# A residual addition moved from VectorE to accumulating transfers on GpSimd's queue

## The chip, the cores and the metric

The kernel runs on one core of a Trainium2 chip. The metric is device time in microseconds (us) for one execution of the whole program; a lower time is better. A core has a matrix engine (TensorE, PE in the profile; PEld is its loading of weights), a vector engine (VectorE, DVE), a scalar engine (ScalarE, ACT), GpSimd (POOL) and a queue engine (SyncE, SP). Each takes its instructions in the order in which the program lists them and waits, in that order, for the semaphores of other engines and of transfers (DMAs). Work is held in SBUF, 128 partitions wide; PE writes to PSUM, of which this kernel uses five accumulator tiles of 128 x 512 (`ACC = 5`).

## The reference

The input x has 4 batches of 1024 rows and 2048 columns. From a small matrix product come six modulation vectors per batch (`sa, ca, ga, sb, cb, gb`). Then two residual steps follow:

```
h = layernorm(x) * (1 + ca) + sa
x = x + ga * conv(h)            # long convolution along the 2048 columns, plus D[0]*h
h = layernorm(x) * (1 + cb) + sb
x = x + gb * (h @ W.T + bias + low-rank update)
```

The change concerns the second line, the addition of x to the gated convolution, and what the layer norm of the third line needs of that sum: its mean and its variance along each row.

## The kernel before

**Stages.** The 4096 rows of x are 32 tiles of 128 rows, numbered r = 0 to 31. In a first stage (about 0 to 190 us) the modulation vectors are computed from `wmod` and the convolution's tables are made; tiles 0 and 1 are convolved there without gate (`EARLY = 2`). In the second stage (about 190 to 912 us) tiles 2 to 31 are convolved, one after the other; a turn of that loop (lines 1143 to 1181) is called block r here. Into the blocks up to about r = 24 the kernel mixes "fill" work: the merge of W with its low-rank update (`merge`, line 483: PE products `lps` at L502, taken from PSUM by VectorE at L504, split by ACT and DVE at L529 and L530, stored as `wcd`) and the remaining modulation sections (`modps`, L320). In the third stage (about 912 us to the end) 16 pairs of tiles go through the feed-forward product (`ffn_unit`, L829), twice, once for each half of the columns.

**One block.** `conv_mm` (line 657) multiplies in two passes, q = 0 and q = 1; q = 1 has 2.6 times the columns of q = 0. Each pass has three families of PE products: family 0 into the PSUM tile `ya`, copied by ACT to `qs` (L695); family 2 into `yb`; family 1, which goes on accumulating in `ya`. VectorE then makes one half of a row's 1024 elements from `yb` (L704: add `qs`; L706: times the row's scale `rsx` and the gate `gat`) and the other half from `ya` (L713: times `rsx` and `gat`, here called the gate of the pass). At L714 VectorE adds x to the 1024 columns of the pass and gives out the row sums through its accumulator (`sums`).

**After a block.** `conv_post` (line 732) of tile r stores y to DRAM (`x1d`, L734), turns the two row sums into minus the mean (L736), and lets ACT square the sum with that bias and accumulate the variance (L739). The squares that ACT gives out are not used; they are written over the x tile, which then is free.

**Buffers.** x has four buffers in SBUF (`x{r % 4}`), y two. So the tile x of r + 3 is loaded (`x_load`, L614) into the buffer of tile r - 1, and its load comes after `conv_post` of r - 1. Of x VectorE makes row statistics (`stats`, L566 `bn_stats`, four instructions a tile, then L567), for two tiles at a time. They end in a small PE product (`qp`, L581), a PE transpose (`svp`, L606) and scales `cas` and `rsx` that the preparation of the tile (`conv_prep`) and its gate need. The transposed copy `xt`, from which the convolution's operand is made, is a separate load (L620).

**What sets the order.** `conv_mm` calls `tick()` at ten places in a block: after each of the six families, and in the middle of each family of pass 1 (numbers 3, 5 and 7), and number 9 after the block. `PLAN` (line 891) has a string for each of them. "P" is `conv_post` of the block before and the load of x for r + 3; "N" a step of the next tile's preparation; "S" a step of fill work; "T" (even r only) the first part of the statistics for r + 2 and r + 3, "t" one of the two later parts (`qp`; then `svp`). The framework places each engine's instructions in one fixed order from this program order and from its own estimates. SP issues all large transfers, in order, with at most eight semaphores in turn; an issue that waits holds up those behind it. POOL's own queue has 28 transfers in the whole kernel, all before 146 us, and a few memsets.

At the end of the second stage, the weights of the second and third product of the third stage are loaded into the four x buffers (`XW`, line 1082): those of the third product (`w5`) into the buffers of tiles 30 and 31.

Of the kernel before, what the change touches and what calls it, by code (L numbers as in the profile page):

```python
# [12 lines left out]
F32 = mybir.dt.float32  # L13
F16 = mybir.dt.float16
BF16 = mybir.dt.bfloat16
I32 = mybir.dt.int32
AF = mybir.ActivationFunctionType
ALU = mybir.AluOpType
AX = mybir.AxisListType
MUL, ADD, SUB = ALU.mult, ALU.add, ALU.subtract  # L20
# [4 lines left out]
P = 128  # L25
D = 2048
# [9 lines left out]
class Net:  # L36
# [515 lines left out]
    def stats(self, pl, rs_, out):  # L552
        nc, v = self.nc, self.nc.vector
        n, b = len(rs_), rs_[0] // 8
        tt = v.tensor_tensor

        def T(shape, name, dt=F32):
            if name in ("cas", "rsx", "sw"):
                return pl["sm1" if n == 1 else "sm"].tile([P, *shape], dt, tag=f"{name}{n}", name=name)
            return pl["sm"].tile([P, 2, *shape[1:]], dt, tag=name, name=name)[:, 0:n]  # L560

        mv = T((n, 2), "mv")
        for i, r in enumerate(rs_):
            st = pl["sm"].tile([P, 4, 6], F32, tag="st1", name="st1")
            for q in range(4):
                v.bn_stats(st[:, q], self.xs[r][:, ds(512 * q, 512)])  # L566
            v.bn_aggr(mv[:, i], st)  # L567
        mean, var = mv[:, :, 0], mv[:, :, 1]
        m2, qb = T((n,), "m2"), T((n,), "qb", BF16)
        tt(m2, mean, mean, MUL)  # L570
        tt(qb, m2, var, ADD)
        ve, t, rs = T((n,), "ve"), T((n,), "t"), T((n,), "rs")
        v.tensor_scalar(ve, var, 0.25, 0.25e-5, MUL, ADD)
        nc.scalar.activation(t, ve, AF.Sqrt)
        v.reciprocal(rs, t)
        tt(ve, ve, rs, MUL)
        tt(var, ve, t, ADD)
        v.reciprocal(rs, var)
        yield
        qp = self.tps.tile([P, n], F32, tag="t", name="qp")  # L580
        self.lastq = nc.tensor.matmul(qp, self.ones, qb, start=True, stop=True)  # L581
        bd = T((n,), "bd")
        nc.scalar.activation(bd, qp, AF.Sqrt, bias=self.tiny, scale=self.cm2[:, b : b + 1])
        inv, s2 = T((n,), "inv"), T((n,), "s2")
        v.tensor_scalar(inv.bitcast(I32), bd.bitcast(I32), 0x7F800000, None, ALU.bitwise_and)
        v.tensor_scalar(s2.bitcast(I32), inv.bitcast(I32), 0x7F800000, None, ALU.bitwise_xor)
        cas, rsx = T((n, NC), "cas"), T((n,), "rsx")
        cab = self.ca[:, :, b].unsqueeze(1).to_broadcast([P, n, NC])
        tt(cas, cab, s2.unsqueeze(2).to_broadcast([P, n, NC]), MUL)  # L589
        tt(rsx, rs, inv, MUL)  # L590
        full = self.spt[rs_[0] // 2 % 2][:, rs_[0] % 2 : rs_[0] % 2 + n]
        if rs_[0] % 8 < 4:
            nc.gpsimd.memset(full, 0.0)
        f3 = full[:, :, ds(18 * b, 18)].rearrange("p n (i k j) -> p n i k j", i=2, k=3)
        w = T((n, 2), "w")
        s2b = s2.unsqueeze(2).to_broadcast([P, n, 2])
        tt(w, mv, s2b, MUL)
        for k in range(3):
            for i in range(n):
                v.tensor_copy(f3[:, i, :, k], w[:, i].unsqueeze(2).to_broadcast([P, 2, 3]))  # L600
            if k < 2:
                tt(w, w, f3[:, :, :, k, 0], SUB)
        yield
        tp = self.tps.tile([P, n, P], BF16, tag="t", name="svp")
        for i in range(n):
            nc.tensor.transpose(tp[:, i], full[:, i], self.identb)  # L606
        sw = T((n, P), "sw", BF16)
        nc.scalar.copy(sw, tp)
        out.update({r: (cas[:, i], rsx[:, i : i + 1], sw[:, i]) for i, r in enumerate(rs_)})
        yield  # L610

    def x_load(self, pl, r):
# [44 lines left out]
    def conv_mm(self, pl, r, hs, x, st, tick, early, pace, hook=None):  # L657
        nc, v = self.nc, self.nc.vector
        hc, hs = hs
        y = yv = None  # L660
        if not early:
            gv = self.gat.rearrange("p (j e t) -> p j e t", e=2, t=P)
            mv = self.gm.rearrange("k (j e t) -> k j e t", e=2, t=P)
        rsx = st[1]
        sums = self.sums[:, r]

        def rank(ps, jj, e):
            if not early:
                nc.tensor.matmul(ps, st[2], mv[:, jj, e, :], start=False, stop=False, skip_group_check=True)

        def family(ps, f, q, first):
            pf = ps.rearrange("p j t -> p (j t)")
            last = 4 * q + 3
            for i in range(last + 1):
                o = P * max(0, i - 4 * q)
                k0 = P * max(0, 4 * q - i)
                with pace(3 * (512 - o)):
                    for x, z in ((0, 0), (0, 1), (1, 0)):
                        h = hs[x][:, i] if f == 0 else hc[x][:, 2 * i + 2 - f]
                        self.lastc = nc.tensor.matmul(  # L680
                            pf[:, o:512], h, self.kf[f][z][:, ds(k0, 512 - o)],
                            start=first, stop=(i == last and (x, z) == (1, 0)), skip_group_check=True,
                        )
                        first = False
                if i == (last - 1 if hook else 0) and f:
                    rank(ps, slice(4 * q, 4 * q + 4), f // 2)
                if i == 3 and q == 1:
                    tick()

        for q in range(2):  # L690
            jj = slice(4 * q, 4 * q + 4)
            pa = self.acc.tile([P, 4, P], F32, tag="a", name="ya")
            family(pa, 0, q, True)
            qs = pl["t"].tile([P, 4, P], F32, tag="qs", name="qs")
            self.lasta = nc.scalar.copy(qs, pa)  # L695
            tick()
            pb = self.acc.tile([P, 4, P], F32, tag="a", name="yb")
            family(pb, 2, q, True)
            if y is None:
                if hook:  # L700
                    hook()
                y = pl["y"].tile([P, D], F32, tag="y", name="y")
                yv = y.rearrange("p (j e t) -> p j e t", e=2, t=P)
            self.lastv = v.tensor_tensor(yv[:, jj, 1, :], pb, qs, ADD)  # L704
            if not early:
                v.scalar_tensor_tensor(yv[:, jj, 1, :], yv[:, jj, 1, :], rsx, gv[:, jj, 1, :], MUL, MUL)  # L706
            tick()
            family(pa, 1, q, False)
            sl = ds(1024 * q, 1024)
            if early:  # L710
                nc.scalar.copy(yv[:, jj, 0, :], pa)
            else:
                v.scalar_tensor_tensor(yv[:, jj, 0, :], pa, rsx, gv[:, jj, 0, :], MUL, MUL)  # L713
                v.scalar_tensor_tensor(y[:, sl], y[:, sl], 1.0, x[:, sl], MUL, ADD, accum_out=sums[:, q : q + 1])  # L714
            tick()
        return y, sums

# [11 lines left out]
            v.scalar_tensor_tensor(y[:, sl], y[:, sl], st[1], self.gat[:, sl], MUL, MUL)  # L729
            v.scalar_tensor_tensor(y[:, sl], y[:, sl], 1.0, x[:, sl], MUL, ADD, accum_out=sums[:, q : q + 1])  # L730

    def conv_post(self, pl, r, x, y):
        nc, v = self.nc, self.nc.vector
        STQ(nc).dma_start(out=self.x1d[r], in_=y)  # L734
        mn = self.ln2[:, r, 0:1]
        v.tensor_scalar(mn, self.sums[:, r, 0:1], self.sums[:, r, 1:2], -1.0 / D, ADD, MUL)  # L736
        if r < EARLY:
            x = pl["mrg"].tile([P, D], BF16, tag="wct", name="lsj")
        nc.scalar.activation(x, y, AF.Square, bias=mn, accum_out=self.sqs[:, r : r + 1])  # L739
        if r % 8 == 7:  # L740
            sl = slice(r - 7, r + 1)
            self.rstd(pl["sm8"], self.sqs[:, sl], self.ln2[:, sl, 1], 8, "r2", 1.0 / D)
            v.tensor_tensor(self.ln2[:, sl, 0], self.ln2[:, sl, 0], self.ln2[:, sl, 1], MUL)
# [144 lines left out]

MR = 2
ACC, TPS = 5, 2  # L890
PLAN = ("PNSL", "NL", "NSL", "NTL", "SL", "StL", "SL", "StL", "SL", "SSL")
PLAN2 = ("", "", "", "", "N", "N", "N", "N", "", "")
PLAN3 = ("PS", "", "S4", "", "NS", "NS", "NS5", "NS", "S", "SS")
LPLAN = ("LL", "LL", "LL", "LL", "L", "0", "")
# [4 lines left out]
EARLY = 2  # L899
# [6 lines left out]
def STQ(nc):  # L906
    return nc.sync
# [7 lines left out]
def net(ctx: ExitStack, tc: tile.TileContext, io):  # L915
    nc = tc.nc
    k = Net(ctx, tc, io)
# [11 lines left out]
    pl = {}  # L929
# [1 line left out]
    msm = pool(right, "msm", 1, "right")  # L931
    pl["x"] = pool(p2, "p1x", 1)
    k.kpool = pool(left, "kt", 1)
    k.sums = k.kpool.tile([P, 32, 2], F32, tag="sums", name="sums")
    k.identb = k.kpool.tile([P, P], BF16, tag="identb", name="identb")
    nc.gpsimd.tensor_copy(k.identb, k.ident)
    k.ones = k.kpool.tile([P, P], BF16, tag="ones", name="ones")
# [54 lines left out]
    xs, xts, hs, sts, ys = {}, {}, {}, {}, {}  # L992
# [148 lines left out]
    post = None  # L1141
    sgen = [iter(())]
    for r in range(EARLY, 32):
# [34 lines left out]
        y, _ = k.conv_mm(pl, r, hs.pop(r), xs[r], sts[r], tick, False, behind if r == EARLY else none, late if r == EARLY else None)  # L1178
        tick()
        take(nxt, 9)  # L1180
        post = (r, xs.pop(r), y)
    k.conv_post(pl, *post)
    take(lgen, 10)
    gens = [next_left(1)]
# [94 lines left out]
```

## Time and profile before

| quantity | value |
|---|---|
| median of the runs shown (3) | 2137.91 us (2133.5 to 2143.52) |
| the profiled execution's own time | 2131.82 us |
| span of that execution in the profile | 2130.0 us, so 1.8 us lie around it |
| granted PE clock over the span | 0.986 of full |
| GpSimd busy | 24.2 us in 53 instructions |
| bytes moved by DMA | 512.97 MB, of it 1.65 MB on GpSimd's queue |

The profile is one execution, taken by the hardware profiler. Busy time counts an engine's instructions; a wait is put down to the semaphore that was raised last. Ends of PE's instructions are modelled, so a busy PE may still wait a little. In the views of groups a row gives line, engine, operation, tiles written and read, shapes and count, then the busy time and the mean duration, then idle time just before and who ended it. In the views of time a row gives start, length, engine, line and tiles. In the views by stretch each row has the stretch, its length, the busy time of PE, PEld, DVE, ACT and POOL with their counts, then the granted PE clock, the share of the 16 DMA engines' time and GB/s.

### The profile page before, as it was taken

The numbers are of one execution on the slowest core, as the hardware profiler recorded it, in microseconds if no ns is written. First come the engines' busy times: TensorE is split into PE (matmuls) and PEld (weight loads), VectorE is DVE, ScalarE is ACT, GpSimd is POOL, SyncE is SP. The second block draws the span as 40 slices with busy tenths as digits, with TensorE's granted clock in tenths as the row PEclk, the third lists the DMA queues.
The fourth block names the chain that finished last, engine by engine and source line by source line (L and its number), as shares of the span: only waits on it lengthen the run. The fifth ranks groups of instructions, "written<-read, shape, count | busy, mean of one in ns | idle before, by whom it ended". The sixth has DMA issues, their size and how long they took to land.

```text
span 2130.0 us, 27798 instructions
## 1 busy us (share of the span) xinstructions
PE 2059.7 (97%) x10845; PEld 991.6 (47%) x10845; DVE 1269.6 (60%) x2226; ACT 889.1 (42%) x1564; POOL 24.2 (1%) x53
## 2 busy tenths in 40 slices
PE   6898899999999999999999999999999999999998
PEld 2343454444444555544555555555444444444444
DVE  5437788888989898655565665665533333332323
ACT  1324866666766776646555555554200000000000
POOL 1020000000000000000000000000000000000000
PEclk7898999999999999999999999999999999999999
DMA  9896858888887675487564664564794545454542
GB/s 404 319 369 259 327 177 329 333 326 321 336 340 296 210 262 200 179 344 253 217 227 170 217 227 169 217 232 164 297 345 158 187 148 181 165 167 159 178 155 70
DMA packets 131954, 512.97 MB, mean 241 GB/s; under 512 B 14432, under 2 KB 14960, under 8 KB 97262
## 3 DMA queue, kind: packets, MB, share of 16 engines
q1 hardware_dynamic: 130224, 506.92, 65.3%
q10 hardware_dynamic: 526, 2.63, 0.3%
q8 instruction: 85, 1.39, 0.3%
q0 software_dynamic: 1072, 1.65, 0.2%
q14 instruction: 47, 0.39, 0.1%
HBM read 355.55 MB, written 155.59 MB: 240 GB/s over the span
## 4 chain that ended last, share of the span: by engine, by line
PE 74%; DMA 8%; DVE 8%; issue 6%; ACT 3%; SPq 0%; POOL 0%; POOLq 0%; ACTq 0%; DVEq 0%
PE fZ L829 23%; PE fY L829 15%; PE fX L829 15%; PE ya L680 8%; PE yb L680 4%; PE modps L320 3%; PE tp L779 2%; PE lps L502 2%; DMA wm<-in_wmod 2%; DMA x<-in_x 1%; DVE wch L530 1%; DVE st L566 1%; DMA xo<-x1d 1%; DMA x<-x1d 1%; DMA gsd<-rkg 1%
## 5 line engine op out<-in xcount | busy, mean ns | idle before, releaser
L829 PEld LDWEIGHTS <-lf 128*128 128x128 f16 x5376 | 525.8, 98 | 620.9 <-issue 1.1
L829 PE MATMUL fZ<-w,lf 128*128 128x512 f16 x2304 | 514.1, 379 | 0.8 <-ACT p L837 0.8
L829 PE MATMUL fY<-w,lf 128*128 128x512 f16 x1536 | 342.1, 379 | 0.0
L829 PE MATMUL fX<-w,lf 128*128 128x512 f16 x1536 | 342.1, 379 | 0.0
L680 PEld LDWEIGHTS <-hc 128*128 128x128 f16 x2304 | 212.4, 98 | 217.2 <-issue 56.4
L847 DVE TENSOR_TENSOR xo<-xo,gb 128x512 f32<-128x512 f32 x128 | 87.4, 689 | 221.1 <-DMA xo<-x1d 208.0
L680 PE MATMUL ya<-kh,hc 128*128 128x512 f16 (+3 forms) x768 | 204.0, 329 | 8.9 <-ACT qs L695 8.9
L680 PE MATMUL yb<-kh,hc 128*128 128x512 f16 (+3 forms) x768 | 202.3, 328 | 1.1 <-DVE y L713 0.8
L680 PE MATMUL ya<-kh,hs 128*128 128x512 f16 (+3 forms) x768 | 189.4, 326 | 1.8 <-ACT hs L629 1.8
L837 ACT COPY p<-fZ 128x512 f32<-128x512 f32 x64 | 37.2, 582 | 293.0 <-PE fZ L829 276.3
L680 PEld LDWEIGHTS <-hs 128*128 128x128 f16 x1152 | 106.1, 98 | 109.1 <-issue 23.4
L781 ACT ACTIVATE gt<-tp,sb,cb 128x256 f32<-128x256 f32 x256 | 123.9, 570 | 65.7 <-PE tp L779 65.7
L837 ACT COPY p<-fX 128x512 f32<-128x512 f32 x32 | 18.7, 585 | 311.4 <-PE fX L829 241.0
L645 ACT ACTIVATE xt<-xt,cas 128x128 f32<-128x128 f32 x448 | 140.1, 392 | 9.0 <-DVE cas L589 9.0
L320 PE MATMUL modps<-wm,sct 128*32 128x512 f32 x768 | 117.7, 653 | 20.6 <-DMA wm<-in_wmod 13.3
L680 PE MATMUL ya<-kl,hc 128*128 128x512 f16 (+3 forms) x384 | 126.0, 328 | 0.0
L680 PE MATMUL yb<-kl,hc 128*128 128x512 f16 (+3 forms) x384 | 126.0, 328 | 0.0
L680 PE MATMUL ya<-kl,hs 128*128 128x512 f16 (+3 forms) x384 | 125.1, 326 | 0.0
L852 DVE TENSOR_TENSOR fin<-fX,gb 128x512 f32<-128x512 f32 x32 | 22.1, 691 | 126.9 <-PE fX L829 126.8
L566 DVE BATCH_NORM_STATS2 st<-x 128x6 f32<-128x512 f32 x128 | 81.5, 680 | 12.2 <-DMA x<-in_x 12.2
L792 DVE TENSOR_TENSOR lf<-gt,lf 128x1024 f16<-128x1024 f32 x64 | 76.7, 1219 | 17.3 <-ACT lf L791 17.2
L502 PE MATMUL lps<-lbh,lac 128*128 128x512 f16 x256 | 87.0, 382 | 0.0
(289 smaller groups left out, 2126.1 us busy)
## 6 DMA issues: line engine op xcount, KB each, us to landing
wm<-in_wmod SPq DMA_DIRECT2D x96, 1024.0 KB
lfd<-lf SPq DMA_DIRECT2D x112, 512.0 KB
lf<-lfd SPq DMA_DIRECT2D x112, 512.0 KB
x<-in_x SPq DMA_DIRECT2D x32, 1024.0 KB
x1d<-y SPq DMA_DIRECT2D x32, 1024.0 KB
x<-x1d SPq DMA_DIRECT2D x32, 1024.0 KB
xo<-x1d SPq DMA_DIRECT2D x128, 256.0 KB
out<-xo SPq DMA_DIRECT2D x128, 256.0 KB
```

The source lines that it names most:

```text
L320: self.last = self.nc.tensor.matmul(self.modps[32 * g : 32 * g + 32, :], self.sct[:, j].rearrange("p r b -> p (r b)"), w[:, ds(512 * g, 512)],
L502: nc.tensor.matmul(ps, la[:, x, k, h], y[:, k, osl], start=(n == 0), stop=(n == 5))
L566: v.bn_stats(st[:, q], self.xs[r][:, ds(512 * q, 512)])
L645: nc.scalar.activation(xt[:, k], src, AF.Copy, scale=cas[:, k : k + 1])
L680: self.lastc = nc.tensor.matmul(pf[:, o:512], h, self.kf[f][z][:, ds(k0, 512 - o)], start=first, stop=(i == last and (x, z) == (1, 0)), sk ...
L779: nc.tensor.transpose(tp[:, c, r], xs[r][:, ds(P * (c0 + c), P)], self.ident)
L781: nc.scalar.activation(t[:, c0 + c], tp[:, c], AF.Identity, bias=self.sb[:, c0 + c, b : b + 1], scale=self.cb[:, c0 + c, b : b + 1],)
L792: v.tensor_tensor(hl[:, :, 1, :], s, hl[:, :, 0, :], SUB)
L829: nc.tensor.matmul(ps[name], lf[i][:, k, x, :], wc[i][k // 4][:, k % 4, y, :], start=(first and n == 0), stop=(n == 3 * HC - 1), skip_grou ...
L837: nc.scalar.copy(t, ps[name])
L847: v.tensor_tensor(x, x, self.gbias[:, h], ADD)
L852: v.tensor_tensor(t, cv, self.gbt[:, h], MUL)
```

## The change

VectorE's addition of x at L714 is gone for tiles 2 to 31. In its place, after the gate of each pass, GpSimd's queue issues a transfer from SBUF to SBUF that adds y to x in place, 128 x 1024 elements, 512 KB, two a tile. The sum so stands in the x tile and not in y: `conv_post` stores x, and ACT squares x and writes its unused squares over y. The row sums now come from accumulators of both gate instructions of a pass (four sums a tile); they are sums of the gated convolution alone, so `conv_post` adds the row mean of x that `stats` has, which is kept for that. `PLAN` is changed as well: P goes from tick 0 to tick 2, T from tick 3 to tick 5, and the two t from ticks 5 and 7 to ticks 7 and 9. Tiles 0 and 1 are treated as before.

```
-        out.update({r: (cas[:, i], rsx[:, i : i + 1], sw[:, i]) for i, r in enumerate(rs_)})
+        out.update({r: (cas[:, i], rsx[:, i : i + 1], sw[:, i], mv[:, i, 0:1]) for i, r in enumerate(rs_)})
...
             if not early:
-                v.scalar_tensor_tensor(yv[:, jj, 1, :], yv[:, jj, 1, :], rsx, gv[:, jj, 1, :], MUL, MUL)
+                v.scalar_tensor_tensor(
+                    yv[:, jj, 1, :], yv[:, jj, 1, :], rsx, gv[:, jj, 1, :], MUL, MUL,
+                    accum_out=sums[:, 2 * q + 1 : 2 * q + 2],
+                )
...
-                v.scalar_tensor_tensor(yv[:, jj, 0, :], pa, rsx, gv[:, jj, 0, :], MUL, MUL)
-                v.scalar_tensor_tensor(y[:, sl], y[:, sl], 1.0, x[:, sl], MUL, ADD, accum_out=sums[:, q : q + 1])
+                v.scalar_tensor_tensor(
+                    yv[:, jj, 0, :], pa, rsx, gv[:, jj, 0, :], MUL, MUL, accum_out=sums[:, 2 * q : 2 * q + 1]
+                )
+                nc.gpsimd.dma_start(out=x[:, sl], in_=y[:, sl], accum_op=ADD)
...
-    def conv_post(self, pl, r, x, y):
+    def conv_post(self, pl, r, x, y, mean=None):
         nc, v = self.nc, self.nc.vector
-        STQ(nc).dma_start(out=self.x1d[r], in_=y)
-        mn = self.ln2[:, r, 0:1]
-        v.tensor_scalar(mn, self.sums[:, r, 0:1], self.sums[:, r, 1:2], -1.0 / D, ADD, MUL)
-        if r < EARLY:
-            x = pl["mrg"].tile([P, D], BF16, tag="wct", name="lsj")
-        nc.scalar.activation(x, y, AF.Square, bias=mn, accum_out=self.sqs[:, r : r + 1])
+        mn, sums = self.ln2[:, r, 0:1], self.sums[:, r]
+        if mean is None:
+            v.tensor_scalar(mn, sums[:, 0:1], sums[:, 1:2], -1.0 / D, ADD, MUL)
+            x, y = y, pl["mrg"].tile([P, D], BF16, tag="wct", name="lsj")
+        else:
+            v.tensor_reduce(mn, sums, AX.X, ADD)
+            v.scalar_tensor_tensor(mn, mn, -1.0 / D, mean, MUL, SUB)
+        STQ(nc).dma_start(out=self.x1d[r], in_=x)
+        nc.scalar.activation(y, x, AF.Square, bias=mn, accum_out=self.sqs[:, r : r + 1])
...
-PLAN = ("PNSL", "NL", "NSL", "NTL", "SL", "StL", "SL", "StL", "SL", "SSL")
+PLAN = ("NSL", "NL", "PNSL", "NL", "SL", "STL", "SL", "StL", "SL", "StSL")
...
-    k.sums = k.kpool.tile([P, 32, 2], F32, tag="sums", name="sums")
+    k.sums = k.kpool.tile([P, 32, 4], F32, tag="sums", name="sums")
...
-        post = (r, xs.pop(r), y)
+        post = (r, xs.pop(r), y, sts[r][3])
```

In the changed file the gate of a pass is L716, the new transfer L719, the store L746 and the square L747.

## The prediction, made before the changed kernel was run

> **What bounds the kernel now.** I read the engine totals first, then the busy time by stretch, PE's waits, VectorE's rows, and one block in order of time.
>
> ```profile
> PE 2059.7 (97%) x10845; PEld 991.6 (47%) x10845; DVE 1269.6 (60%) x2226; ACT 889.1 (42%) x1564; POOL 24.2 (1%) x53
> ```
>
> PE bounds the whole. VectorE's 60% is a mean over stages, so the stretches of the second stage matter, where the change works:
>
> ```profile
> 215.00:400.00 185.00, 174.78 (x1015) 84.79 (x1014) 154.34 (x315) 129.11 (x244) 1.32 (x3) 0.97 0.77 283
> 400.00:560.00 160.00, 155.83 (x928) 74.78 (x927) 136.18 (x267) 103.21 (x202) 0.62 (x2) 1.00 0.88 333
> 560.00:680.00 120.00, 119.05 (x717) 57.80 (x716) 108.13 (x220) 84.02 (x164) 0.62 (x2) 1.00 0.85 323
> 680.00:790.00 110.00, 104.13 (x614) 55.76 (x611) 101.01 (x204) 81.45 (x157) 2.45 (x1) 1.00 0.68 239
> 790.00:912.00 122.00, 119.22 (x736) 67.27 (x735) 95.80 (x175) 79.31 (x150) 0.00 (x0) 1.00 0.54 199
> ```
>
> VectorE is busy 78 to 92% here (595.45 of 697 us) and the DMA engines 54 to 88%, but PE is busy 673 of 697: all that a relief of VectorE can win is within PE's 24 idle us. PE's waits (total, times, longest) between 215 and 915 us name less:
>
> ```profile
> PE qp L581 <- DVE qb L571: 10.2, 8, 1.9
> PE modps L320 <- DMA wm<-in_wmod: 5.4, 2, 3.7
> PE ya L680 <- ACT qs L695: 3.2, 2, 2.8
> PE svp L606 <- DVE spt L600: 3.2, 7, 0.7
> ```
>
> On VectorE PE waits 14.4 us in all (10.2 + 3.2, and 1.0 in two short waits for y and we). Block 10 shows where the 10.2 comes from:
>
> ```profile
> 386.65 0.75 DVE L713 SCALAR_TENSOR_TENSOR y<-ya,rsx,gat 128x512 f32<-128x512 f32 x1
> ```
> ```profile
> 393.71 0.46 SPq L734 DMA_DIRECT2D x1d<-y  x1
> 394.26 0.77 SPq L614 DMA_DIRECT2D x<-in_x  x1
> ```
> ```profile
> 404.08 2.48 DVE L566 BATCH_NORM_STATS2 st<-x 128x6 f32<-128x512 f32 x4 [3.49 <-DMA x<-in_x]
> ```
> ```profile
> 408.25 0.16 PE L581 MATMUL qp<-qb,ones 128*128 128x2 bf16 x1 [1.90 <-DVE qb L571]
> ```
>
> Block 9's gate ends at 387.40; its store and the load of x13 are issued 6.3 and 6.9 us later; VectorE stands 3.49 us until x13 lands at 404.08 (load 9.8), and PE then 1.9 for qp. So the tightest thing beside PE is a ring: gate of r-1, buffer free, load of x for r+3, its statistics, and then, since VectorE works in order, the gate of r.
>
> **VectorE's work.** What goes and what changes:
>
> ```profile
> L714 DVE SCALAR_TENSOR_TENSOR y<-y,x 128x1024 f32<-128x1024 f32 x60 | 73.1, 1218 | 0.6
> L714 DVE DVE_READ_ACCUMULATOR y<-y,x 128x1 f32 x60 | 4.9, 82 | 0.0
> L706 DVE SCALAR_TENSOR_TENSOR y<-y,rsx,gat 128x512 f32<-128x512 f32 x60 | 44.4, 741 | 0.4
> ```
>
> Removed: 73.1 + 4.9 = 78.0. Added: an accumulator read behind each of 120 gates, 120 x 0.082 = 9.8; in `conv_post` two small operations of about 0.2 (L736's row) for one, 30 x 0.2 = 6. Net -62 us of 595, some 2 us a block. It stands beside PE, so it is worth at most PE's 14.4 us of waits on VectorE. An accumulator on the gates may cost more than its read: L714 carries one and takes 1.218 for 1024 elements, as the plain addition L530 (1.22), so I take 0; the other end, the difference of L713's 745 and L704's 683, is 0.06 x 120 = 7, beside PE as well. The Trainium skill ("Vector Engine (DVE) Microarchitecture Reference", section 7, points that are easy to get wrong) says that this two-tensor form with two SBUF sources that are not bf16 runs at half throughput; then a gate from y would cost about double the one from PSUM. The rows differ by 4 ns (741, 745) and L714 goes at the plain addition's pace, so the row decides.
>
> **The ring with the change.** The x tile is no longer free when ACT's square is done: the store reads it. So before the load of x for r+3 come, in series, (a) the accumulation behind the gate, A; (b) the store of x, and the load waits until that has landed. The store is issued by SP, so the load and all of SP's later transfers (xt, wm, we, wcd) queue behind both waits. S and load have rows: pairing each issue with its semaphore's last increment from 215 to 800 us, the x1d store has a median of 6.8 us (3.8 to 13.4) and the x load 6.8 (4.9 to 12.5).
>
> A has no row of its kind. GpSimd's queue shows:
>
> ```profile
> kb<-kd POOLq DMA_DIRECT2D x1, 1024.0 KB, 9.8
> gsd<-rkg POOLq DMA_DIRECT2D x24, 12.0 KB, 5.1
> gm<-gsd POOLq DMA_DIRECT2D x1, 288.0 KB, 7.8
> ```
>
> From below: the fastest of the gsd transfers, 3.4. From above: 9.8, twice the bytes on a busy bus (DMA share 0.84 to 0.89 there). Nearest in size, 7.8 for 288 KB; but it goes through DRAM, and small ones take 5.1 to 5.4. I take **6.5**, between. The Trainium skill ("DMA: Bandwidth & Descriptors", SWDGE path of the anatomy of one DMA) fits 2.0 us + bytes / 436e3 per us, so an estimate of 3.2 us for 512 KB, and would speak for the first rival; 12 KB should then take 2.0, and this trace has 5.1.
>
> The fixed leg from gate to x in SBUF is 0.3 (issue) + 6.5 + 6.8 + 6.8 = 20.4 us. In block 10 x13 would land at 407.8 in place of 404.08. The tail, from bn_stats to the end of block r's gate in VectorE's order of the changed kernel, is for block 10: four L566 2.72, L567 0.26, seven small ones 1.16, L704 0.68, L706 0.82, four L504 2.98, ten small ones 1.66, gate 0.83, and 0.5 for ACT's root, 11.6 us. 20.4 + 11.6 - 26.7 (gate to gate before) = 5.3 us late. PE carries about 4: three spare PSUM tiles, each a fill product of six matmuls, 1.3 us. So lateness adds up from block to block (down to 0), and what exceeds 4 is a stall of PE. Tail / period for the others, summed likewise: 5: 5.1/32.8; 6: 14.2/25.3; 7: 2.2/25.0; 8: 7.9/31.7; 11: 12.2/28.1; 12: 3.5/24.0; 13: 6.5/29.7; 14: 8.6/26.0; 15: 4.3/24.9; 16: 12.3/28.1; 17: 3.5/22.1; 18: 10.1/29.4; 20: 14.1/27.3; 21: 7.6/24.9; 22: 9.6/23.4; 23: 5.8/24.7; 24: 12.9/22.2; 9 and 19 have no such wait and start at 0. Stalls: block 6 5.3, 10 1.3, 11 4.6, 14 0.1, 16 4.4, 17 1.8, 18 1.1, 20 3.2, 21 3.1, 22 6.6, 23 1.5, 24 11.0, together **+44 us**. In blocks 25 to 28 the DMA share is lower and tails are 4 to 6 of 19 to 21: 0. The same sum gives +12 for A = 3.4, +25 for 5.1, +69 for 7.8, +108 for 9.8.
>
> **The rest.** GpSimd: 60 issues of 0.51 to 0.57 (its rows), 33 us on an idle engine: 0. Its queue's next transfer waits a whole pass; nothing else uses it then. DMA: two transfers add 256 rows of 4 KB a block; at 0.171 us a packet (mean of SP's queue) on 16 engines that is 2.7 us a block, double if the add reads twice, so 0.1 to 0.2 of share; its price is within A's upper end. P is moved from tick 0 to 2, but the store was issued 6.3 us behind the gate in block 10 anyway, and now at 6.8: 0.5, in the sum. T and t are two ticks later; `svp` follows the block, so a late x reaches the next block's preparation; in the tails. The square of ACT now waits for the accumulation; in the built order those of tiles 10, 15 and 17 stand ahead of the next block's qs copy (L695), which PE needs: up to 5 us each, in blocks 11, 16 and 18, where 10.1 us of stalls already stand; 0, at most +5.
>
> **End of the stage.** `w5` goes into the x buffers of tiles 30 and 31: its second half now waits for the accumulation and the store of tile 31. Before:
>
> ```profile
> 914.61 6.14 SPq L1093 DMA_DIRECT2D w<-wcd  x9
> ```
>
> It landed at 920.4 and PE needed it at 923.8. With A 6.5, the store's 5.2 and the load's 5.8 of that place (gate end near 910.9) it lands at about 928.4: **+5** (0 to 10), after which the third stage stands unchanged.
>
> **Sum.** 2131.8 (the profiled execution; the median shown is 6 us above) + 44 + 5 = 2181 us. What would speak against it: blocks whose tail is shortened as VectorE has 62 us less to do; the tails have that already.
>
> **Rivals.** (1) Faster: A is 3.4 to 4 and stores land in under 6, so x13 lands by 404 as now. No stall is added, the tails are 2 us shorter, and PE's 14.4 us of waits go: 2131.8 - 14.4 + 3 at the end = 2120. For it: VectorE at 78 to 92%; against: the store's median alone is as long as the slack. It decides from A + S below about 9. (2) About the same: A near 4, +14 in the stalls, -14.4 returned, +3: 2135. (3) More than slower: the bus at 0.88 fills up, A reaches 9.8 and blocks 5 to 24 run on the ring: 2131.8 + 108 + 8 = 2248. For it: 0.88 and 0.85 from 400 to 680; against: 0.54 to 0.68 after. (4) The offload does not do what it says: accumulators cost VectorE 7 and the squares PE 5 more on the forecast, 2186 to 2193.
>
> **Numbers.** Chances: forecast with (4) 0.48 (2150 to 2215), (1) 0.20, (2) 0.14, (3) 0.18. Half a per cent is 10.7 us, about what a measurement of this kernel can tell from no change. Of (2), 0.12 lies within it and 0.02 above. Faster 0.20, same 0.12, slower 0.68. The range, 2115 to 2250, takes in both ends of A.
>
> **What would show it.** After: x loads issued only once a store has landed, some 14 us behind the gate; waits of `st` for x on VectorE well above 11.2 us; PE's waits on qb or y growing in blocks 6, 10, 11, 20 to 24, and none from 25; DVE busy about 62 us lower. An accumulation that lands in 4 us, or loads that are issued in time by other free buffers, would make it wrong.

## The result, and the profile after

The changed kernel takes 2257.98 us (median of 4 runs, 2256.93 to 2260.16) against 2138.27 before in the same sessions: 1.056 times as long, 95% interval 1.0535 to 1.0587. The forecast was 2181 with a range up to 2250: slower as forecast, but by 120 us and not by 43 (its sum adds 49 to an execution of 2131.8). Totals and the two largest DMA queues (queue, packets, MB, share of 16 engines' time) of the changed kernel:

```profile
PE 2095.1 (93%) x10845; PEld 1002.9 (44%) x10845; DVE 1214.2 (54%) x2256; ACT 890.2 (39%) x1564; POOL 74.3 (3%) x113
q1 hardware_dynamic: 130224, 506.92, 62.4%
q0 software_dynamic: 9712, 33.11, 7.4%
```

VectorE does 55 us less, as intended. PE, with the same 10845 matmuls, is busy 35 us longer. GpSimd's queue (q0) has gone from 0.2% to 7.4%: 0.072 x 2258.2 / 60 is 2.7 us of all 16 DMA engines for each 512 KB transfer. The stretches of the second stage, which now ends at 1034 us and not at 912:

```profile
215.00:400.00 185.00, 159.56 (x877) 75.39 (x876) 116.93 (x289) 109.53 (x215) 11.29 (x15) 0.93 0.84 281
400.00:560.00 160.00, 142.89 (x832) 68.60 (x831) 109.59 (x223) 96.97 (x181) 9.46 (x13) 0.97 0.95 316
560.00:680.00 120.00, 94.22 (x529) 44.97 (x528) 84.31 (x177) 65.36 (x129) 5.95 (x7) 0.89 0.91 301
680.00:790.00 110.00, 102.05 (x591) 50.17 (x589) 73.04 (x167) 61.22 (x126) 6.58 (x9) 0.96 0.84 279
790.00:912.00 122.00, 104.01 (x584) 54.69 (x583) 93.72 (x205) 81.96 (x148) 9.83 (x11) 0.96 0.86 271
```

Three columns tell it: PE idles 17 to 26 us a stretch where it idled 1 to 10 (only from 680 to 790 us no more than 8, 6 before); the granted clock (third from the end) is 0.89 to 0.97 where it was 0.97 to 1.00; the DMA share (last but one) is 0.84 to 0.95. Nearly all of the loss is in this stage: by the ends of the second-pass gates, block 4 is done at 262.6 us in place of 247.5, blocks 5 to 24 take 614.8 in place of 525.4, blocks 25 to 30 128.9 in place of 118.4, block 31 27.6 in place of 19.7, and from there to the end it is 1224.3 in place of 1219.1.

Who waits, in the views of PE's, ACT's and SP's waits (total, times, longest) from 215 to 1045 us; of ACT's 91.9 us the longest, 13.2, is tile 31's, behind the last block:

```profile
PE ya L680 <- ACT qs L695: 43.1, 13, 8.5
PE qp L581 <- DVE qb L571: 23.7, 6, 7.4
PE lps L502 <- DVE y L704: 10.1, 2, 6.2
```
```profile
ACT y L747 <- DMA x<-y: 91.9, 19, 13.2
```
```profile
SPq L746 <- DMA x<-y: 260.2, 29, 17.2
...
SPq L614 <- DMA x1d<-x: 89.3, 23, 10.5
```

The wait that the forecast looked for (qp) is there, 23.7 where it was 10.2. The larger one is another: PE waits for ACT's copy `qs`, and ACT for the accumulation. SP stands 260 us for the accumulation at the store and 89 for the store's landing at the load of x. One scene, after block 15, in order of time (start, length, engine, line): GpSimd issues the second transfer of the block; SP's issues; ACT; PE.

```profile
601.66 0.85 POOL L719 DMA_DIRECT2D x<-y  x1 [18.89 <-DVE ln L744]
```
```profile
613.48 0.33 SPq L746 DMA_DIRECT2D x1d<-x  x1
613.91 0.37 SPq L315 DMA_DIRECT2D wm<-in_wmod  x1
618.63 0.33 SPq L614 DMA_DIRECT2D x<-in_x  x1
619.05 0.38 SPq L620 DMA_DIRECT2D xt<-in_xT  x1
```
```profile
613.49 2.00 ACT L747 ACTIVATE y<-x,ln 128x2048 f32<-128x2048 f32 x1 [8.04 <-DMA x<-y]
...
615.49 0.56 ACT L695 COPY qs<-ya 128x512 f32<-128x512 f32 x1
```
```profile
616.11 0.58 PE L680 MATMUL ya<-kh,hc 128*128 128x512 f16 x1 [8.54 <-ACT qs L695]
```

The transfer takes 11.8 us here. Until it lands, SP holds the store and, behind it, `wm`, x and `xt`; ACT holds the square and, behind it, `qs`; PE stands 8.54 us. Afterwards PE doesn't come back at full speed (view by stretch of the changed kernel, before and after this wait):

```profile
590.00:607.00 17.00, 17.00 (x100) 7.97 (x99) 13.84 (x24) 9.06 (x22) 0.85 (x1) 1.00 0.94 356
616.10:619.50 3.40, 3.39 (x12) 1.56 (x12) 2.43 (x7) 1.61 (x4) 0.00 (x0) 0.50 0.95 328
```

The granted clock is 0.50 here, and by narrower stretches until 620.0. The 3.9 us of work at half rate lose some 2 us (an estimate, 3.9 x 0.5), so this wait costs its length and some 2 us more.

### The profile page after: what moved, and what is told of

Same layout as the page of the kernel before. It is cut to its first block, busy times and chain, and to the rows that moved or that the text cites. A ratio compares the mean times of both kernels' runs of the same rounds, so it can differ in the third digit from the quotient of the medians.

```text
span 2258.2 us, 27995 instructions
## 1 busy us (share of the span) xinstructions
PE 2095.1 (93%) x10845; PEld 1002.9 (44%) x10845; DVE 1214.2 (54%) x2256; ACT 890.2 (39%) x1564; POOL 74.3 (3%) x113
## 4 chain that ended last, share of the span: by engine, by line
PE 60%; DMA 17%; issue 11%; DVE 8%; ACT 3%; POOL 1%; SPq 0%; POOLq 0%; ACTq 0%; DVEq 0%
PE fZ L837 21%; PE fX L837 14%; PE fY L837 14%; DMA x<-y 6%; PE ya L680 3%; PE tp L787 3%; DMA wcd<-wch 2%; PE yb L680 2%; DMA we<-in_WT 2%; DMA x1d<-x 1%; DMA x<-in_x 1%; PE modps L320 1%; DMA laf<-in_A 1%; DVE wch L530 1%; DVE st L566 1%
## 5 line engine op out<-in xcount | busy, mean ns | idle before, releaser
L680 PEld LDWEIGHTS <-hc 128*128 128x128 f16 x2304 | 219.5, 101 | 276.7 <-issue 120.6
L680 PE MATMUL ya<-kh,hc 128*128 128x512 f16 (+3 forms) x768 | 215.1, 345 | 48.9 <-ACT qs L695 48.9
L680 PE MATMUL ya<-kh,hs 128*128 128x512 f16 (+3 forms) x768 | 197.4, 336 | 8.9 <-DVE y L704 4.1
L789 ACT ACTIVATE gt<-tp,sb,cb 128x256 f32<-128x256 f32 x256 | 124.3, 571 | 67.8 <-PE tp L787 67.6
L680 PE MATMUL ya<-kl,hc 128*128 128x512 f16 (+3 forms) x384 | 132.3, 345 | 0.0
L502 PE MATMUL lps<-lbh,lac 128*128 128x512 f16 x256 | 89.0, 391 | 14.9 <-DVE y L704 10.1
L747 ACT ACTIVATE y<-x,ln 128x2048 f32<-128x2048 f32 x30 | 60.1, 2002 | 101.7 <-DMA x<-y 93.1
L630 DVE TENSOR_TENSOR hc<-xt,hc 128x1024 f16<-128x1024 f32 x64 | 78.1, 1222 | 40.4 <-ACT hc L629 40.0
L566 DVE BATCH_NORM_STATS2 st<-x 128x6 f32<-128x512 f32 x128 | 81.7, 681 | 30.5 <-DMA x<-in_x 30.5
```

Of the source, the lines that this page charges most:

```text
L502: nc.tensor.matmul(ps, la[:, x, k, h], y[:, k, osl], start=(n == 0), stop=(n == 5))
L630: v.tensor_tensor(pair[1][:, sl], src, pair[0][:, sl], SUB)
L680: self.lastc = nc.tensor.matmul(pf[:, o:512], h, self.kf[f][z][:, ds(k0, 512 - o)], start=first, stop=(i == last and (x, z) == (1, 0)), sk ...
L747: nc.scalar.activation(y, x, AF.Square, bias=mn, accum_out=self.sqs[:, r : r + 1])
L789: nc.scalar.activation(t[:, c0 + c], tp[:, c], AF.Identity, bias=self.sb[:, c0 + c, b : b + 1], scale=self.cb[:, c0 + c, b : b + 1],)
```

## Experiments

Three theories. **Ring**, that of the prediction: accumulation, store and load put x late. **Held queues**: ACT and SP, which work in order, are held by instructions that wait for the accumulation. **DMA time**: 162 us more of the 16 engines (60 x 2.7) slow every other transfer, whoever waits. All runs are in us, with their ratio to the kernel before in the same session.

**e1_relief**: the transfer is left out of the change, y stored and squared, old PLAN.

```
-                nc.gpsimd.dma_start(out=x[:, sl], in_=y[:, sl], accum_op=ADD)
```

> The addition of x is left out altogether (no transfer and no VectorE addition; y alone is stored and squared), with the old PLAN and the row sums from the gates: what VectorE's relief is worth by itself. All theories that put the loss on the transfer or on what waits for it: 2120 to 2138 us, DVE busy about 62 us under 1270, PE's waits on qb down from 10.2. If the accumulators on the gates cost more than their read, or the relief shifts something else: above 2145.

2127.24 (0.9944, 0.9923 to 0.9966). The relief with its accumulators is worth 11 us (5 to 16 by the interval); with all else as here, no way of adding x could win more. The loss from 2127 to 2258 is 131.

**e4_plan**: the kernel before with `PLAN = ("NSL", "NL", "PNSL", "NL", "SL", "STL", "SL", "StL", "SL", "StSL")`.

> The kernel before with the new PLAN alone (P at tick 2, T at 5, t at 7 and 9). Both theories: within 11 us of before, 2127 to 2149. Rival: the later P and t make x and the scales late by themselves, 2155 to 2180.

2139.38 (1.0013, 0.9997 to 1.0028). The new PLAN alone costs nothing.

**e2_nosq**: no square for tiles 2 to 31.

```
+        if mean is None:
             nc.scalar.activation(y, x, AF.Square, bias=mn, accum_out=self.sqs[:, r : r + 1])
```

> The changed kernel without ACT's squares of tiles 2 to 31 (the variance of the second layer norm is left out, a constant stands for it); accumulation, store and load wait as before. ACT theory (squares that wait for the accumulation hold ACT's copies qs and hc that PE and VectorE need): most of the 43 us of PE's waits on qs and what follows from them goes, 2175 to 2205 us. Ring theory of the prediction (accumulation, store, load of x, statistics): nearly nothing, 2240 to 2258.

2231.69 (1.0443, 1.0416 to 1.0469): 26 us less, between the two theories. Part of what was won at `qs` came back at x. PE's and VectorE's waits of this run:

```profile
PE qp L581 <- DVE qb L571: 54.2, 12, 8.8
PE ya L680 <- ACT qs L695: 18.2, 9, 3.7
```
```profile
DVE st L566 <- DMA x<-in_x: 91.6, 21, 9.0
```

In the changed kernel these were 23.7, 43.1 and 30.5. A wait that is taken away uncovers the one beside it.

**e3_reverse**: x is added to y, so that the load of x need not wait for the store.

```
-                nc.gpsimd.dma_start(out=x[:, sl], in_=y[:, sl], accum_op=ADD)
+                nc.gpsimd.dma_start(out=y[:, sl], in_=x[:, sl], accum_op=ADD)
```

> The transfer goes the other way: x is added to y in place, y is stored and squared, and the squares go over x, as in the kernel before; PLAN new. The x buffer no longer waits for the store's landing, only for the accumulation and the square. Ring theory: the store's 4.9 us (median after) leave the ring in about 20 blocks and a 2 us square comes in, 2190 to 2225 us. ACT theory: the square waits for the accumulation as it did, 2240 to 2260.

2249.47 (1.0519): 9 us less; the ring theory asked for 33 to 68.

**e7_revlate**: as e3, and the square moved to tick 7, over y in place.

```
+        self.nc.scalar.activation(y, y, AF.Square, bias=mn, accum_out=self.sqs[:, r : r + 1])
```

> Both waits taken away together: x is added to y by the transfer, y is stored (so no store stands between the x buffer and its load), and ACT's square is moved from tick 2 to tick 7 and writes over y, so that it no longer waits for the accumulation in front of qs and no longer holds the x buffer. If the ring and the held ACT are two bounds side by side, each of which alone hides the other's removal (2232 and 2249 us): 2135 to 2170. If the loss is the transfers' load on the bus or SP's queue held by the waiting store: still 2200 to 2245.

2240.93 (1.0473). A miss for the two bounds: both "taken away" and 103 us of loss left. Part of it is the edit's own: a square in place waits for the landing of y's store, and ACT still stood 65.6 us for that between 215 and 985 us. **e11_rev_nosq**, e3 without the squares, is the clean form:

> The reversed transfer (x added to y) without ACT's squares (the variance is left out): neither the store nor the square stands between x's buffer and its load, and ACT waits for no transfer. If the 57 us above traffic alone (2258 against 2201) are these two waits: 2195 to 2215. If SP's queue, held 240 us by the store that waits for the accumulation, makes a part of it: 2220 to 2235.

2233.47 (1.0451), within the range for SP's held queue and the same as e2_nosq's 2231.69. So the store's landing in the ring costs nothing more beside the other waits. **e12_rev_nosq_poolstore** gives e11's store to GpSimd's queue (`nc.gpsimd.dma_start(out=self.x1d[r], in_=y)`):

> As e11_rev_nosq with the store issued on GpSimd's own queue, behind the accumulations, so that SP's queue waits for no accumulation but through x's load (the variance is left out). SP theory: 15 us or more under e11_rev_nosq, about 2200. Two-waits theory: within 10 us of e11_rev_nosq.

2264.57 (1.0605), 31 slower than e11 and outside both expectations. It tells little of SP, which now stood 227 us at the load of x for the same accumulation.

**e8_traffic**: e1 plus 60 accumulating transfers that no engine waits for.

```
+                nc.gpsimd.dma_start(out=self.junk[r][:, sl], in_=y[:, sl], accum_op=ADD)
```

> The kernel without any residual addition (2127 us) plus 60 accumulating transfers of the same 512 KB on GpSimd's queue that nobody waits for but the next use of the y buffer: y is added to scratch in DRAM, behind the gate of each pass (the addition of x is left out; the target is DRAM and not SBUF). The price of traffic and queue alone. If waits are the whole loss: 2127 to 2142. If the bus or the queue is: 2180 or more.

2200.68 (1.0286, 1.0262 to 1.0309): 73 us more than e1 for traffic alone. The forecast had nothing for it. **e9_trafcopy**, the same without `accum_op`:

> As e8_traffic, but the transfers that nobody waits for are plain copies of y to scratch in DRAM (the addition of x is left out). In the changed kernel GpSimd's queue takes 2.7 us of all 16 DMA engines a transfer, with plain copies 1.3 (shares 7.4% and 3.8%). If DMA engine time is what traffic costs: half of it or less, 2140 to 2165 us. If the queue or GpSimd's issuing costs, whatever the transfer is: 2190 to 2205.

2164.15 (1.0127, 1.0109 to 1.0144): 37, half. **e5_copy** does that to the changed kernel, waits and all:

> The changed kernel with the transfer as a plain copy of y over x (the addition is left out), same queue, bytes and waits. If reading the target for the addition is what makes the transfer 7.8 us long: it lands in 4 to 6 us and the kernel is 20 to 50 us faster than 2258. If the queue and the fixed part make it: 7 to 8 us again and 2245 to 2260.

2194.51 (1.0258; two executions), 63 under the change; the transfer lands in 6.4 us (median) in place of 7.8, nearer to the first expectation than to the second, and the kernel gains more than its 20 to 50.

**e6_half**: pass 0 by transfer, pass 1 by VectorE.

```
+                if q == 0:
+                    nc.gpsimd.dma_start(out=x[:, sl], in_=y[:, sl], accum_op=ADD)
+                else:
+                    v.tensor_tensor(x[:, sl], y[:, sl], x[:, sl], ADD)
```

> Only pass 0 is added by a transfer; VectorE adds pass 1 into the x tile (which is stored, new PLAN, square over y). The accumulation then lands well ahead of the block's end, so neither store nor square waits for one; the load still waits for the store. Two-bounds theory: 2140 to 2165 (half of the relief, ring 1.2 + 6.8 + 6.8). If the number of transfers counts: half of the loss, 2190 to 2205.

2169.26 (1.0146, 1.0117 to 1.0175). Less than half of the loss: half of the traffic, ACT waits for no accumulation and SP 33 us at the store in place of 260 (but still 79 at x's load for the store's landing). Between the two expectations.

**e10_pooladd**: `nc.gpsimd.tensor_tensor(y[:, sl], y[:, sl], x[:, sl], ADD)` in place of the transfer.

> The addition on GpSimd itself (y = y + x as an instruction of GpSimd, no transfer), old PLAN, sums from the gates: the same relief of VectorE without DMA. Full addition, and the only way left to 2127. If GpSimd adds 128 x 1024 in under 3 us and VectorE isn't slowed by it: 2125 to 2140. If its addition is long, or the two slow each other: 2150 to 2220.

2186.63 (1.0236), in the range of the second expectation. GpSimd's own addition takes 2.68 us, within the first, but VectorE's instructions with two inputs in SBUF get longer (rows of this run; before, 1218 and 683):

```profile
L719 POOL TENSOR_TENSOR y<-y,x 128x1024 f32<-128x1024 f32 x60 | 160.8, 2680 | 595.4 <-DVE y L716 418.3 <-DVE y L706 65.3 <-DVE w L602 27.8
```
```profile
L630 DVE TENSOR_TENSOR hc<-xt,hc 128x1024 f16<-128x1024 f32 x64 | 103.6, 1621 | 14.6 <-ACT hc L629 14.0
L630 DVE TENSOR_TENSOR hs<-xt,hs 128x512 f16<-128x512 f32 x64 | 62.8, 989 | 7.1 <-ACT hs L629 6.8
```

The Trainium skill ("SBUF — State Buffer", who interferes with whom) says that a VectorE instruction with two SBUF inputs contends with a GpSimd instruction that reads SBUF. These rows agree: of the 64 subtractions into `hc`, the 27 that overlap an addition take 2178 ns on average, the other 37 1214, and the one-input L566 stays at 681 in 18 overlaps.

**e13_free** and **e14_free_hold**: as e11, with the gate tile added to y (`in_=self.gat[:, sl]`), so that nothing of x waits; x is loaded at tick 0; the store is put at tick 6 in e13 and at tick 2 in e14.

> The same 60 accumulating transfers from SBUF to SBUF, but nothing of x hangs on them: they add the gate tile to y (the addition of x is left out, and the squares, so the variance, too), x for r+3 is loaded at tick 0 into a buffer that is free, and the store of y is moved to tick 6, when the accumulation has landed. DMA engine time is then all that is left: as the transfers into DRAM nobody waited for, 2185 to 2210 us. If the transfers cost by waits only: 2120 to 2150.

> As e13_free with the store back at tick 2, so that SP's queue is held at it until the accumulation has landed, some 240 us in all, with the loads and stores of the fill work behind it; x's load stands ahead of it at tick 0 (addition of x and squares left out). If SP's held queue makes the rest of the loss: 15 us or more above e13_free, towards 2233. If it was x's late load: within 8 us of e13_free.

2221.12 (1.0401), outside both expectations, and 2223.77 (1.0419). The two can't be told apart for a reason of their own: the framework put the store early in SP's order in both, and SP stood for it 243 us in e13 and 249 in e14 between 215 and 985 us. **e15_late_post** has P at tick 4 in the full changed kernel:

> The changed kernel in full with P (store, square, load of x for r+3) at tick 4 in place of 2. SP and ACT are then held less by the accumulation, but x is loaded later. If holding SP and ACT is the larger part of the 57 us above traffic: 2225 to 2250. If x's load is: 2258 to 2290.

2237.57 (1.0481): 20 less than the change, with ACT's wait for the accumulation down from 91.9 to 44.9 us. SP stood nearly as long as before at store and load (239 and 85 us; 260 and 89 in the change), so the later P relieved ACT above all, by more than the later load of x cost.

**e16_unawaited, e17_unawaited_none, e18_unawaited_copy**: e14 with the store sending the gate tile, so that in the second stage neither engines nor SP's stores of x1d wait for one of the transfers: with accumulation, without any transfer, with a plain copy.

```
-        STQ(nc).dma_start(out=self.x1d[r], in_=y)
+        STQ(nc).dma_start(out=self.x1d[r], in_=self.gat)
```

> As e14_free_hold, but the store sends the gate tile in place of y, so that no engine and no queue waits for the accumulating transfers at all (the addition of x and the squares are left out, the stored tile isn't the sum). In e13_free the store still stood early in SP's queue and held it 243 us, so that e13 and e14 didn't differ in it. If SP's held queue made part of e13's 2221: 2180 to 2205. If it is DMA engine time alone: 2212 to 2225.

> As e16_unawaited without any transfer: the base for the price of the transfers by themselves. No squares on ACT, no addition: 2115 to 2130 in every theory.

> As e16_unawaited with plain copies of the gate tile over y (half the DMA engine time a transfer, and same number, bytes and issues). DMA-engine-time theory: its distance to e17_unawaited_none is half of e16's or less. If the number of transfers or GpSimd's issuing counts: the same distance as e16.

2190.38 (1.0258), 2128.68 (0.9962) and 2150.64 (1.0073). The transfers cost 62 us with the addition and 22 as copies, with the same number, bytes and issues. What differs is the DMA engines' time, and it makes the 40 between them; for the 22 of the copies, number and issues are not ruled out. (SP's three loads of the gate tile itself do wait for transfers that read it, 30 us in all in e16 and 27 in e18, and behind the second stage of e16 one copy of ACT waits 15.4 us for the last transfer; that is not taken away. Up to the last gate alone, the profiled executions take 903.4 us in e17, 928.3 in e18 and 960.4 in e16: +25 and +57.) GpSimd's queue in e16, then e18:

```profile
q0 software_dynamic: 9712, 33.11, 7.6%
```
```profile
q0 software_dynamic: 9712, 33.11, 3.9%
```

That is 2.7 and 1.3 us of 16 engines for 512 KB. The rows from 215 to 900 us of e17, e18 and e16:

```profile
215.00:900.00 685.00, 666.91 (x3993) 338.32 (x3992) 528.98 (x1200) 421.73 (x857) 3.08 (x8) 1.00 0.77 287
215.00:900.00 685.00, 653.13 (x3845) 327.73 (x3844) 513.15 (x1178) 407.15 (x841) 31.64 (x62) 0.98 0.86 323
215.00:900.00 685.00, 627.49 (x3627) 311.40 (x3626) 494.29 (x1137) 383.17 (x784) 45.51 (x58) 0.97 0.94 320
```

The DMA share is 0.77, 0.86 and 0.94, and the medians of the others' landings go up from e17 to e16: `wm` 7.0 to 9.8 us, `xt` 6.1 to 8.5, `wcd` 3.8 to 5.2, x 9.7 to 12.7. VectorE's instructions are not longer (L530 1218 and 1220 ns). The Trainium skill ("Collectives: The Full Stack", the bandwidth ceiling) says of the add in a ring's ReduceScatter that it needs two source reads; the ratio of 2.0 for this accumulation would fit that.

**The sum along this path**, each step one thing more:

| step | runs | us |
|---|---|---|
| no addition of x, no squares, no transfers | e17 | 2128.7 |
| accumulating transfers, nobody waits | e16 | +62 |
| the store in SP's queue waits for them | e14 | +33 |
| x's load waits too | e11 | +10 |
| and for the store's landing | e2 | -2 |
| ACT's square waits, in front of `qs` | after | +26 |

Squares that wait for no transfer show no cost (e1 with them 2127.2, e17 without 2128.7; the two differ in PLAN and in what is stored, too). Each size holds in this order only: what comes late finds part of its price already paid, as e2 showed. The +10 and the -2 are within the scatter: the intervals of e14 (1.0399 to 1.0438), e11 (1.0428 to 1.0475) and e2 (1.0416 to 1.0469) overlap, and e14 has 39 us of SP's waits at the loads of the gate tile that e11 has not. The store in e16 doesn't wait for VectorE's gates either, nor does that of its base e17.

## Why the prediction was right in sign and wrong in size

Part of the waits that it named were there. What failed is the price of the transfers' DMA time, which it took to lie in A: it fell on all other transfers (+62). Next come the ACT square (+26) and SP's held queue (+33), put at nothing or nearly so, while the ring, which carried its +44, added 10 at most.

- **VectorE's relief, at most 14.4 us of PE's waits**: right; 11 by e1. Busy time fell by 55, forecast 62.
- **The accumulators on the gates**: right at 0. Both forms take 746 ns (741 and 745 before) and an 83 to 84 ns read:

```profile
L706 DVE SCALAR_TENSOR_TENSOR y<-y,rsx,gat 128x512 f32<-128x512 f32 x60 | 44.8, 746 | 0.8
L716 DVE SCALAR_TENSOR_TENSOR y<-ya,rsx,gat 128x512 f32<-128x512 f32 x60 | 44.8, 746 | 18.4 <-PE ya L680 18.1 <-PE qp L581 0.2
```

- **A, 6.5 us within 3.4 to 9.8**: measured 7.8 (median), the value of its 288 KB row. The estimate of 3.2 from the skill's fit was far too low here. S was 4.9 and x's load 6.1 against 6.8 each, so the leg is 0.3 + 7.8 + 4.9 + 6.1 = 19.1, forecast 20.4. The ring's length was right, with luck: A was longer, store and load shorter.
- **The ring's price, +44 (69 by its table at 7.8)**: wrong; at most some 10 for the load and nothing for the store's landing, once the costs of DMA time and SP's queue stand. Its table took all else as unchanged. The sign it gave fits only in part: VectorE's waits for x grew from 11.2 to 30.5 us, but PE's waits on `qb` (23.7 us) stand before the second-pass gates of blocks 4, 13, 15, 24, 26 and 28, and not in 6, 10, 11, 20 to 24 with none from 25. (Redone from the tails that it prints, the sum is 44 at 6.5, but 64 at 7.8 and 94 at 9.8, not 69 and 108.)
- **"its price is within A's upper end", of the DMA time**: this step failed most. The forecast had the time right, 2.7 us a block and double if the add reads twice, 5.4 measured. But it charged it only to A. The idle share was 0.12 to 0.23 from 215 to 680 us, and the time fell on all other transfers, whose landings got later: +62 with A in nobody's way. Of these, e18 shows 40 to be DMA engine time.
- **SP's later transfers "queue behind both waits"**: seen, and priced at nothing; +33.
- **The square, "0, at most +5"**: +26. ACT stood for the accumulation 19 times and not in three blocks, PE for `qs` 13 times: in blocks 11 (4.1 us) and 16 (8.5, not 5) of the three named, and also in 6 to 8, 10, 14, 17, 22, 24, 26 and 31.
- **The clock**: no term at all. From 215 us to the end of the second stage PE is busy 709.8 us in place of 673.0, with 4026 records and 4004. By the clock's record the rate is at half for 99 us there, 10 before, and PE is busy in 74 and 9 of them: a loss of 37 and 4 us (an estimate, half of the busy time). So about 33 of the 122 us by which the stage grew are PE working slower, not waiting; they are part of the steps above and not beside them.
- **End of the stage, +5**: the time from the last gate to the end grew by 5.2, so the size was right, but by luck. PE has no wait for `w` there; it stood 3.5 us for ACT's `gt` (L789), which came behind tile 31's square and its wait of 13.2 us, and then worked 3.4 us at half rate.
- **Rival (3)**, 2248, came nearest in time and had the share of 0.88 as its reason, but put all of it on A and the ring: near by luck.
- **GpSimd's issues, 33 us at no price**: its busy time rose by 50, 0.85 us an issue in the scene above; GpSimd had nothing else to do.

What stays open: how the 62 us divide among late `xt`, `we`, `wm`, `wcd` and x was not separated, nor what part of the 22 us of plain copies is the engines' time.

## What to carry to other kernels

Charge a transfer that is added to a busy stage to the DMA engines first: time per transfer, times their number, against the idle share of that stage; an accumulating one took twice a copy's time here. Then list each instruction that will wait for it and what stands behind that instruction in its engine's order, on SP and ACT as well as on the engine that was relieved, since several such waits cover each other, and removing one shows little. Before moving work off an engine, leave the work out and time that: here it was worth 11 us, which bounds what any new place for it can win; none of the full versions run here beats the kernel before (the nearest, e6_half, takes 1.0146 of its time, some 30 us more).

## What the runs showed of the hardware

- In the scene after block 15 PE stood 8.5 us from 607.6. The granted clock was 1.00 until 609.8, then 0.50 until 620.0, so for 3.9 us of work, then 1.00. The Trainium skill ("TensorE: Matmul & The Clock Gate", part 1) has half rate after an idle window of about 3.4 us and until about as long of work. The length agrees; but here the rate fell 2.2 us into the wait, and elsewhere after a wait of only 2.1 us (PE idle from 873.8 to 875.9, 0.50 from 876.1 to 879.5).
- An SBUF to SBUF accumulation of 512 KB took 2.7 us of all 16 DMA engines, a copy 1.3, and landed in 7.8 and 6.4 us (medians of the changed kernel and e5; 10.1 and 8.4 in e16 and e18).
- GpSimd adds 128 x 1024 in 2.68 us, and VectorE's 1218 ns subtraction took 1621 on average in that run, 2178 where the two overlap.
